# The last shared slot of each block gathered over 112 partitions instead of 128

## The chip, the cores and the metric

The kernel runs on one core of one Trainium2 chip. A time is device microseconds (us) of one execution. The kernel before was run six times: median 799.03 us, lowest 793.24, highest 803.08.

## The reference

Two graph layers run over the same 4096 nodes of 512 features and the same adjacency matrix, which is random with a density of about 1/1024 (four neighbours per node on average). Layer 0 is an attention layer with 8 heads of 64, layer 1 is a mean over the neighbours; each ends in a residual and a layer norm. Cut to what matters:

```python
# layer 0, per head h
Wh = jnp.einsum('nf,hfo->hno', x, W)
f1 = jnp.einsum('hno,ho->hn', Wh, a[:, :F_OUT])
f2 = jnp.einsum('hno,ho->hn', Wh, a[:, F_OUT:])
e = leaky_relu(f1[:, :, None] + f2[:, None, :], 0.2)
e = jnp.where(adj[None] > 0, e, -9e15)
out = jnp.einsum('hnm,hmo->hno', softmax(e), Wh)
x = layernorm(x + out)
# layer 1
agg = mask @ x / max(deg, 1)
combined = concat([x @ W_self + b_self, agg @ W_nb + b_nb])
x = layernorm(x + relu(combined @ W_comb + b_comb))
```

## The kernel before

Nodes are cut into 32 blocks of 128, one node per partition. The kernel never multiplies by the adjacency matrix: it turns each row of it into a list of neighbours and fetches the neighbours' rows from a table in device memory.

**Lists (up to about 225 us of the span).** The adjacency matrix is read block by block. `decode` (L455) turns four blocks at a time into lists. The first three neighbours of each node (K0 = 3) get slots 0 to 2, one row per partition. All further neighbours of a block go, one after the other, into a list shared by the block, of at most 256 entries (KH = 2 times 128): entries 0 to 127 are slot 3, entries 128 to 255 are slot 4, the last shared slot. For each entry the kernel keeps the row to fetch (`idx`), the owner (the node it belongs to, in `es`) and the owner's score part `f1` (`f1s`, copied from PSUM in L523). An entry past the end of its block's list has no owner and fetches row 0 of the table, whose scores are -1e30, so that its weight is zero. Meanwhile the rows of table `t0` (8 scores and 512 features per node) are computed and stored.

**The attention stage (to about 486 us).** For each block, `gather` (L622) issues five indirect DMAs on POOL's queue, one per slot; each fetches one row per partition into the block's tile `g`. All are recorded on L613, the one line of the helper `rows_of` (L612). There are GA = 5 such tiles, each made by `gather_buffer` (L618), so the gathers of block b+5 wait until block b is used up: slot 0 by L668, slots 1 and 2 by L685 on DVE, and slots 3 and 4 by the matmuls of `a_shared` (L697 on PE), which add shared entries to their owners. DVE weighs the rows (L663), ACT scales the sums (L713), makes the layer norm (L728 to L737) and copies what PE made out of PSUM (L351, L746). The products for layer 1 are stored to table `t1` and the transposed features to `xt`.

**The second stage (from about 530 us).** The same lists are used again on rows of `t1`. There are GB = 7 tiles `g`: the five of before and two new ones made at L1078, after the tiles of the list stage were given back. Gathers of blocks 0 to 5 whose rows are ready are issued early (`gather_early`, L629; six late ones follow, `gather_late`, L632). Weights of layer 1 are folded by PE and ACT (`fold_weights`, L296). In the loop, PE multiplies `xT` (reloaded on SP's queue, L769) by the folded weight (`g_self`, L774) and adds the shared slots (`g_shared`, L781); DVE adds slots 1 and 2 (L759, L761) and closes the block (`g_moments`, L797 and L801); ACT makes the norm; SP's queue stores the result (L809). A block's reuse of a tile waits for ACT (slot 0), DVE (1 and 2) and PE (3 and 4).

The order on every engine is the program's order, written by hand. The first tile is made just before the gather of block 0 (L970), the second before that of block 1 (L983), three more before that of block 2 (L987). A test at L1115 sets a flag if some block's shared list is longer than 256 entries; then a dense version of both layers runs after this one.

Of the kernel before, what the change touches and what calls it, by code (L numbers as in the profile page):

```python
# [31 lines left out]
F32 = mybir.dt.float32  # L32
# [4 lines left out]
OP = mybir.AluOpType  # L37
# [3 lines left out]
P = 128  # L41
SLOPE = 0.2
EPS = 1e-5
BIG = 1e30
# [5 lines left out]
K0 = 3  # L50
KH = 2
KS = K0 + KH
KL = 16
KX = KL - K0
GA = 5
GB = 7
NE = 6
# [2 lines left out]
G = 4  # L60
# [26 lines left out]
@with_exitstack  # L87
def kernel(
    ctx: ExitStack,
    tc: tile.TileContext,  # L90
    x: bass.AP,
    adj: bass.AP,
    w0: bass.AP,
    a0: bass.AP,
    w_self: bass.AP,
    b_self: bass.AP,
    w_nb: bass.AP,
    b_nb: bass.AP,
    w_comb: bass.AP,
    b_comb: bass.AP,  # L100
    out: bass.AP,
):
    nc = tc.nc
    flag_pool = ctx.enter_context(tc.tile_pool(name="flag", bufs=1))
    flag = flag_pool.tile([1, 1], I32, name="flag")
    listed_layers(tc, flag, x, adj, w0, a0, w_self, b_self, w_nb, b_nb, w_comb, b_comb, out)
    fl = nc.values_load(flag[0:1, 0:1])
    with tc.If(fl > 0):
        dense_layers(tc, x, adj, w0, a0, w_self, b_self, w_nb, b_nb, w_comb, b_comb, out)
# [3 lines left out]
def listed_layers(  # L113
# [15 lines left out]
    nc = tc.nc  # L129
    N, FIN = x.shape  # L130
    H, _, D = w0.shape
# [6 lines left out]
    TW = H + HD  # L138
# [6 lines left out]
    NC = 32  # L145
    EX = KX + 2 + 1
    AHEAD = (6, 13)
# [8 lines left out]
    const = ctx.enter_context(tc.tile_pool(name="const", bufs=1))  # L156
# [20 lines left out]
    pidx = const.tile([P, KH], F32, name="pidx")  # L177
    nc.gpsimd.iota(
        pidx, [[P, KH]], base=0, channel_multiplier=1, allow_small_or_imprecise_dtypes=True
    )  # L180

    scale = const.tile([P, 1], I32, name="scale")
    nc.gpsimd.iota(scale, [[0, 1]], base=0, channel_multiplier=1)
# [59 lines left out]
    f1s = const.tile([P, NB, KS, H], F32, name="f1s")  # L243
    idx = const.tile([P, NB, KS], U32, name="idx")
    deg = const.tile([P, NB], F32, name="deg")
    end = const.tile([P, NB], F32, name="end")
# [208 lines left out]
    def decode(b0, dp, place):  # L455

        bs = slice(b0, b0 + G)
# [57 lines left out]
        pe = ps.tile([P, G, KH, EX + H], F32, name="sm", bufs=2)  # L515
        for g in range(G):
# [3 lines left out]
                    start=True, stop=True,  # L520
                )
        nc.vector.tensor_copy(es[:, bs], pe[:, :, :, 0:EX])
        nc.vector.tensor_copy(f1s[:, bs, K0:KS, :], pe[:, :, :, EX:])  # L523
        kx = dp.tile([P, G, KH], F32, name="kx", bufs=1)
        nc.vector.tensor_tensor(
            kx, pidx.unsqueeze(1).to_broadcast([P, G, KH]), es[:, bs, :, KX], OP.subtract
        )
        jk = dp.tile([P, G * KH, KX], F32, name="jk", bufs=1)
        nc.vector.tensor_tensor(
            jk, iota[:, 0:KX].unsqueeze(1).to_broadcast([P, G * KH, KX]),  # L530
            kx.rearrange("p g k -> p (g k)").unsqueeze(2).to_broadcast([P, G * KH, KX]),
            OP.is_equal,
        )
        nc.vector.tensor_mul(
            jk, jk, es[:, bs].rearrange("p g k c -> p (g k) c")[:, :, 0:KX]
        )
# [75 lines left out]
    def rows_of(out, table, at):  # L612
        nc.gpsimd.indirect_dma_start(  # L613
            out=out, out_offset=None, in_=table,
            in_offset=bass.IndirectOffsetOnAxis(ap=at, axis=0),
        )

    def gather_buffer(k):  # L618
        pool = ctx.enter_context(tc.tile_pool(name=f"gat{k}", bufs=1))
        return pool.tile([P, KS, TW], F32, name="g")  # L620

    def gather(table, b, g, at=None):  # L622
        for k in range(KS):
            rows_of(
                g[:, k, 0 : table.shape[1]], table, (idx if at is None else at)[:, b, k : k + 1]
            )
        return g

    def gather_early(b, pool):  # L629
        return gather(t1[0 : 2 + min(LE + b, LX) * P, :], b, pool, idxe)  # L630
# [61 lines left out]
    def a_shared(b):  # L692

        for a in range(2):
            r = slice(a * (H + HH), H + HH + a * HH)
            for k in range(KH):
                nc.tensor.matmul(  # L697
                    NM[b][:, a * HD : a * HD + r.stop - r.start],
                    lhsT=OWN[b][:, k, :], rhs=G0[b][:, K0 + k, r],
                    start=False, stop=(k == KH - 1), skip_group_check=True,  # L700
                )
# [225 lines left out]
    for b in range(LB - 1):  # L927
        for k in range(1 + (b in AHEAD)):
            load_x(w + k + XL)
        load_adj(b + 2, ap)  # L930
        if b == 4:
            pads(wp)
        for k in range(2):
            some(lists)
        for k in range(1 + (b in AHEAD)):
            nxt = transposed(w + 1, wp, sums)
            if k == 0 and b in (22, 23, 24):
                transposed(EARLY + b - 22, wp, sums, True)
            if k == 0:
                key_bank(b + 1)  # L940
                for h in range(NH):
                    mask_adj(b + 1, h)
            node_block(w, xT, None if k else b)
            w, xT = w + 1, nxt
        for k in range(2):
            some(lists)
        if b == 16:
            lates = late_lists(dp, fp.tile([P, FB * HD // P, P], F32, name="wr"))
        if b >= 16:
            next(lates, None)  # L950
        if b == 25:
            pieces = mean_row(w_sb, sums, xa)
        if b >= 25:
            next(pieces, None)
        if b % G == G - 1:
            lists = [decode(b + 1 - G, dp, on_own)]
# [11 lines left out]


    gps = [gather_buffer(0)]  # L970
    G0[0] = gather(t0, 0, gps[0])
    mask_adj(LB, 1)
    key_bank(LB + 1)
# [7 lines left out]
    max_keys(LB + 1)  # L981
    ap_cm.__exit__(None, None, None)
    gps.append(gather_buffer(1))  # L983
    G0[1] = gather(t0, 1, gps[1])
    bp_cm.__exit__(None, None, None)
    wq = ctx.enter_context(tc.tile_pool(name="work2", bufs=1))
    gps += [gather_buffer(k) for k in range(2, GA)]  # L987

    def place(c):
# [18 lines left out]
    for k in range(9):  # L1008
        some(lists)
    lists = [decode(NB - G, dp, on_last)]  # L1010
    for k in range(5):
        next(m2s)


    def on(b):
        return 0 <= b < NB
# [3 lines left out]
    for i in range(-3, NB + 2):  # L1020
        if on(i + 1):
            a_shared(i + 1)
        if on(i + 1 + GA):
            G0[i + 1 + GA] = gather(t0, i + 1 + GA, gps[(i + 1 + GA) % GA])
        elif on(i + GA - NB - 1) and i + GA - NB - 1 < GA:
            b = i + GA - NB - 1
            G1[b] = gather_early(b, gps[(NB + b) % GA])
        if on(i + 3):
# [79 lines left out]
    bad = small.tile([P, 4, NB], F32, name="bad", bufs=1)  # L1108
# [3 lines left out]
    )  # L1112
    nc.vector.tensor_scalar(bad[:, 0, :], bad[:, 0, :], FMAX, None, OP.is_gt)
    nc.vector.tensor_scalar(bad[:, 1, :], fmax[:, :, 0], FMAX, None, OP.is_gt)
    nc.vector.tensor_scalar(bad[:, 2, :], end, float(KH * P), None, OP.is_gt)  # L1115
    nc.vector.memset(bad[:, 3, :], 0.0)
    nc.vector.tensor_scalar(bad[:, 3, 0:NE], endl, float(P), None, OP.is_gt)
    nc.vector.tensor_reduce(bsum[:, 0:1], bad.rearrange("p a b -> p (a b)"), AX.X, OP.add)
# [429 lines left out]
```

## Time and profile before

| | us |
|---|---|
| median of six runs | 799.03 |
| lowest and highest | 793.24, 803.08 |
| the profiled execution | 791.82 |
| its span, first to last instruction | 790.1 |
| POOL busy, of it the 326 gathers | 345.0, 311.8 |
| PE, ACT, DVE busy | 627.6, 488.3, 479.0 |
| first and last gather start | 225.70, 749.75 |
| data moved | 209.63 MB, 94.39 MB of it on the queue that POOL fills |

The page is one execution. Its busy times are sums over stages that have different limits, so the stages are read one by one. An instruction's "idle before" is the time its engine did nothing just before it, followed by what ended that. Of the 326 gathers, 160 belong to the attention stage, 30 are early and 6 late ones of the second stage, and 130 belong to blocks 6 to 31 there; every fifth of a block (64 in all) is one of the last shared slot.

### The profile page before, as it was taken

To read this page: it belongs to the slowest core of one execution; us is meant where nothing else is said; L and a number is where in the kernel's file an instruction comes from. 1 tells how busy PE (TensorE), PEld (TensorE's weight loads), DVE (VectorE), ACT (ScalarE), POOL (GpSimd) and SP (SyncE) were. 2 spreads that over 40 slices of the span, in tenths; PEclk is the share of its full clock that TensorE was granted. 3 is DMA by queue.
4 is the path that set the end of the run, shared out by engine and by line. 5 is a ranking of instruction groups with operands and counts; after the bars stand their busy time and mean duration, and the time that the engine had idled before them with its cause. 6 is when DMAs were issued, how large, how long until landed. Compare 5 with 4: busy or idle time off the path is not lost.

```text
span 790.1 us, 8945 instructions
## 1 busy us (share of the span) xinstructions
PE 627.6 (79%) x2229; PEld 351.9 (45%) x2230; DVE 479.0 (61%) x1335; ACT 488.3 (62%) x1236; POOL 345.0 (44%) x410
## 2 busy tenths in 40 slices
PE   5789989978953778799777989767499778987894
PEld 2567666756721344445444545423144333333341
DVE  5267879988851388887967778412026433444463
ACT  3687777887730278798877879731045544555564
POOL 4011111111147266565656652647326666676600
PEclk9899999999956789999999999978599999898997
DMA  8999999998997278789777874857438777887741
GB/s 277 406 408 409 407 408 408 409 409 324 359 299 208 73 198 248 241 292 300 239 246 235 240 227 163 270 173 248 129 96 271 237 264 252 277 258 255 253 141 58
DMA packets 92037, 209.63 MB, mean 265 GB/s; under 512 B 13694, under 2 KB 13702, under 8 KB 91978
## 3 DMA queue, kind: packets, MB, share of 16 engines
q1 hardware_dynamic: 63024, 114.05, 39.3%
q0 software_dynamic: 28624, 94.39, 39.1%
q10 hardware_dynamic: 330, 0.54, 0.2%
q8 instruction: 20, 0.33, 0.2%
q14 instruction: 39, 0.32, 0.1%
HBM read 175.25 MB, written 33.69 MB: 264 GB/s over the span
## 4 chain that ended last, share of the span: by engine, by line
PE 28%; ACT 19%; another core or an unknown queue 10%; issue 8%; DVE 4%; DMA 1%; SPq 0%; ACTq 0%; DVEq 0%
PE nm L774 7%; ACT yp L713 6%; PE pw L774 6%; PE pw L781 3%; PE pw L742 3%; PE nm L781 3%; ACT xs L737 3%; ACT xs L728 2%; PE pw L304 2%; ACT xT L351 2%; PE tp L304 1%; ACT ln_rs L731 1%; DMA xT<-xt 1%; DVE g L663 1%
## 5 line engine op out<-in xcount | busy, mean ns | idle before, releaser
L613 POOL DMA_INDIRECT g<-t,idx x290 | 277.5, 957 | 186.4 <-issue 74.4
L742 PE MATMUL pw<-wr,xT 128*128 128x512 f32 x256 | 126.2, 639 | 26.3 <-ACT xT L351 24.9
L420 ACT ACTIVATE ab<-at 128x2048 bf16<-128x2048 int32 x64 | 122.3, 1912 | 37.2 <-DMA at<-in_adj_dram 33.5
L366 PE MATMUL pw<-w_sb,xT 128*128 128x264 f32 x512 | 132.5, 405 | 11.9 <-DVE sums L355 5.0
L366 PEld LDWEIGHTS pw<-w_sb,xT 128*128 128x128 f32 x512 | 95.4, 196 | 40.9 <-issue 7.0
L663 DVE TENSOR_TENSOR g<-g,ew 128x1024 f32<-128x1024 f32 x64 | 77.4, 1210 | 25.8 <-ACT ew L653 25.4
L742 PEld LDWEIGHTS pw<-wr,xT 128*128 128x128 f32 x256 | 50.6, 204 | 87.9 <-issue 58.9
L377 POOL COPY f1s<-lst 128x24 f32<-128x24 f32 x32 | 7.3, 229 | 178.0 <-DVE fmax L374 95.1
L713 ACT ACTIVATE yp<-num,rd 128x64 f32<-128x64 f32 x256 | 73.1, 286 | 15.0 <-DVE rd L705 4.5
L697 PE MATMUL num<-g,own 128*128 128x264 f32 (+1 forms) x256 | 66.2, 404 | 18.8 <-issue 9.3
L774 PE MATMUL nm<-m,xT 128*128 128x512 f32 x128 | 65.0, 655 | 13.5 <-DMA xT<-xt 9.0
L774 PE MATMUL pw<-m,xT 128*128 128x512 f32 x128 | 62.6, 635 | 10.9 <-DMA xT<-xt 7.3
L797 DVE SCALAR_TENSOR_TENSOR sm<-y,lst,nm 128x512 f32<-128x512 f32 x16 | 12.1, 753 | 93.6 <-PE nm L791 43.4
L697 PEld LDWEIGHTS num<-g,own 128*128 128x128 f32 x256 | 48.3, 198 | 30.5 <-issue 11.9
L774 PEld LDWEIGHTS nm<-m,xT 128*128 128x128 f32 x128 | 26.6, 211 | 49.7 <-issue 33.0
L345 PE MATMUL tp<-ident,xs 128*128 128x128 f32 x256 | 40.8, 284 | 7.6 <-DVE sums L355 7.0
L687 DVE TENSOR_TENSOR num<-num,g 128x512 f32<-128x512 f32 x64 | 44.8, 699 | 2.2
L774 PEld LDWEIGHTS pw<-m,xT 128*128 128x128 f32 x128 | 25.8, 204 | 45.4 <-issue 31.6
L345 PEld LDWEIGHTS tp<-ident,xs 128*128 128x128 f32 x256 | 31.6, 147 | 32.3 <-issue 17.4
L613 POOL DMA_INDIRECT g<-t,idxe x30 | 28.5, 951 | 31.7 <-DVE num L681 12.2
L797 DVE SCALAR_TENSOR_TENSOR sm<-y,lst,pw 128x512 f32<-128x512 f32 x16 | 12.1, 754 | 44.4 <-PE nm L781 12.9
L746 ACT COPY row<-pw 128x512 f32<-128x512 f32 x32 | 18.7, 584 | 31.5 <-remote 21.1
(214 smaller groups left out, 996.9 us busy)
## 6 DMA issues: line engine op xcount, KB each, us to landing
at<-in_adj_dram SPq DMA_DIRECT2D x64, 1024.0 KB
xt<-xT SPq DMA_DIRECT2D x32, 256.0 KB
t<-row SPq DMA_DIRECT2D x32, 256.0 KB
xT<-xt SPq DMA_DIRECT2D x32, 256.0 KB
out_dram<-row SPq DMA_DIRECT2D x32, 256.0 KB
t<-row POOLq DMA_DIRECT2D x31, 260.0 KB
xs<-in_x_dram SPq DMA_DIRECT2D x31, 256.0 KB
g<-t,idx POOLq DMA_INDIRECT x290
```

The source lines that it names most:

```text
L345: nc.tensor.transpose(tp[:, c, :], xs[:, b, ts(c, P)], ident)
L366: nc.tensor.matmul(pw, lhsT=xT[:, c, :], rhs=w_sb[:, c, k * HW : (k + 1) * HW], start=(c == 0), stop=(c == FB - 1),)
L420: nc.scalar.activation(ab, loads.pop((b, h)), AF.Relu, accum_out=asum[:, b, h : h + 1])
L613: nc.gpsimd.indirect_dma_start(out=out, out_offset=None, in_=table, in_offset=bass.IndirectOffsetOnAxis(ap=at, axis=0),)
L663: nc.vector.tensor_tensor(gv, gv, E[b][:, sl].unsqueeze(3).to_broadcast([P, sl.stop - sl.start, H, D]), OP.mult,)
L687: nc.vector.tensor_add(halves_of(NM[b]), halves_of(NM[b]), G0[b][:, k, H:TW].rearrange("p (a c) -> p a c", a=2),)
L697: nc.tensor.matmul(NM[b][:, a * HD : a * HD + r.stop - r.start], lhsT=OWN[b][:, k, :], rhs=G0[b][:, K0 + k, r], start=False, stop=(k == KH ...
L713: nc.scalar.mul(Y[b][:, h * D : (h + 1) * D], NM[b][:, o : o + D], RD[b][:, h : h + 1])
L742: nc.tensor.matmul(pz, lhsT=xT[:, c, :], rhs=m2[:, c, :], start=(c == 0), stop=(c == FB - 1))
L774: nc.tensor.matmul(NM[b], lhsT=xT[:, c, :], rhs=m1[:, c, :], start=False, stop=(c == FB - 1), skip_group_check=True,)
L781: nc.tensor.matmul(NM[b], lhsT=OWN[b][:, k, :], rhs=g[:, K0 + k, 0:HD], start=False, stop=(k == KH - 1), skip_group_check=True,)
L797: nc.vector.scalar_tensor_tensor(yp, Y[b], lst[:, b, KL + 1 : KL + 2], NM[b], OP.mult, OP.add)
```

## The change

The last shared slot is fetched for partitions 0 to 111 only. Its last sixteen rows in each tile are set to zero once, when the tile is made (a memset on POOL of partitions 96 to 127, 520 values each; partitions 96 to 111 are then overwritten by the gathers), and stay zero. The `f1` of those sixteen entries gets -1e30 added, from a small constant tile `void`, so that their weight is zero; the copy of L523 becomes an addition for that. The limit of the test on the shared lists falls from 256 to 240 entries.

```diff
+PL = 112
...
+    void = const.tile([P, KH], F32, name="void")
+    nc.vector.tensor_scalar(void, pidx, float((KH - 1) * P + PL), -BIG, OP.is_ge, OP.mult)
...
-        nc.vector.tensor_copy(f1s[:, bs, K0:KS, :], pe[:, :, :, EX:])
+        nc.vector.tensor_tensor(
+            f1s[:, bs, K0:KS, :], pe[:, :, :, EX:],
+            void.unsqueeze(1).unsqueeze(3).to_broadcast([P, G, KH, H]), OP.add,
+        )
...
     def gather_buffer(k):
         pool = ctx.enter_context(tc.tile_pool(name=f"gat{k}", bufs=1))
-        return pool.tile([P, KS, TW], F32, name="g")
+        g = pool.tile([P, KS, TW], F32, name="g")
+        nc.gpsimd.memset(g[96:P, KS - 1, :], 0.0)
+        return g
 
     def gather(table, b, g, at=None):
         for k in range(KS):
+            p = PL if k == KS - 1 else P
             rows_of(
-                g[:, k, 0 : table.shape[1]], table, (idx if at is None else at)[:, b, k : k + 1]
+                g[0:p, k, 0 : table.shape[1]], table,
+                (idx if at is None else at)[0:p, b, k : k + 1],
             )
         return g
...
-    nc.vector.tensor_scalar(bad[:, 2, :], end, float(KH * P), None, OP.is_gt)
+    nc.vector.tensor_scalar(bad[:, 2, :], end, float((KH - 1) * P + PL), None, OP.is_gt)
```

## The prediction

> **What bounds the kernel now.** I read the page first, then the gathers by stage, then the chain of waits and POOL's timeline inside the longest stage.
>
> ```profile
> PE 627.6 (79%) x2229; PEld 351.9 (45%) x2230; DVE 479.0 (61%) x1335; ACT 488.3 (62%) x1236; POOL 345.0 (44%) x410
> ...
> PE 28%; ACT 19%; another core or an unknown queue 10%; issue 8%; DVE 4%; DMA 1%; SPq 0%; ACTq 0%; DVEq 0%
> ```
>
> By busy share PE looks like the bound and POOL (44%) is idle most of the time; POOL is not even in the chain. Both readings mislead. The gathers alone (L613) by stage; columns are the stretch, its length, POOL busy with gathers, PE's granted clock, DMA share, GB/s:
>
> ```profile
> 0.00:225.00 225.00, 0.00 (x0) 0.97 1.01 382
> 225.00:262.00 37.00, 24.50 (x25) 0.59 0.72 219
> 262.00:486.00 224.00, 129.41 (x135) 0.95 0.75 230
> 486.00:586.00 100.00, 48.45 (x51) 0.83 0.57 179
> 586.00:753.00 167.00, 109.40 (x115) 0.92 0.80 256
> ```
>
> To 225 us the DMA engines are full (share 1.01) with the adjacency matrix, and there are no gathers. From then on a gather takes POOL 0.95 us, and 0.30 us pass before the next starts even when nothing is waited for, so the true pace is 1.25 us: 115 gathers in the last stage need 144 of its 167 us. PE needs less there: the chain shows 3.43 us (L774) and 1.72 us (L781) per block, 5.15, against 5 x 1.25 = 6.27 for a block's gathers. POOL paces that stage. Its pauses, with SP's queue and DVE at the same moment (start, length, instruction, idle before):
>
> ```profile
> 666.62 0.96 POOL L613 DMA_INDIRECT g<-t,idx  x1 [0.30 <-issue]
> ...
> 670.43 0.32 SPq L769 DMA_DIRECT2D xT<-xt  x1
> 670.52 0.76 DVE L797 SCALAR_TENSOR_TENSOR sm<-y,lst,pw 128x512 f32<-128x512 f32 x1 [8.60 <-remote]
> 670.72 0.94 POOL L613 DMA_INDIRECT g<-t,idx  x1 [3.14 <-remote]
> ```
>
> and the chain there:
>
> ```profile
> 657.72 12.72 another core or an unknown queue
> 670.43 2.82 DMA xT<-xt
> ```
>
> SP, DVE and POOL wait for different things and are all released within 0.3 us. What they share is PE's completion signal. The trace's semaphore events show it: from 605 to 736 us POOL runs 15 gathers in a row (18.5 us), pauses 3.1 to 3.25 us, runs 15 again, with a period of 21.7 us (the first of the seven pauses is 2.61 us). While it runs, PE finishes 8 to 14 instructions that signal; of these 0 or 1 arrive in most runs, and the rest arrive together 2.8 to 2.95 us after POOL's last gather. So the "unknown queue" of the chain is PE's signals coming late while POOL issues gathers without a break. The same stands at 259.74 (ACT L308 waits 12.77 us, released 2.2 us after a run of 25 gathers from 225.70 to 257.51) and at 567.26 (after a run of 26). I can't see the cause, only the rule: where POOL runs on, others wait until it stops. POOL's gather time is therefore on the path from 225 to 750 us, whatever its busy share.
>
> **The change, part by part.**
>
> *Does it do what it says?* The flag would send everything through the dense layers if a shared list were longer than 240. Counted from the reference's inputs, the longest of the 32 lists has 227 entries, the next 211. The test costs the same and the dense path stays off: 0 us.
>
> *The list stage.* `void` is one DVE instruction of 2 values per partition; L525 (8 values) takes 162 ns. Eight copies of 64 values (L523, 214 ns each) become additions; the nearest addition (jk, 104 values) takes 268 ns, so at most 0.05 us more each, 0.4 us in all. Most of it lies under the full DMA engines before 225 us, and nobody is recorded as waiting for L523. If uncovered: 0.5 us. I take 0.
>
> *Memsets, five before or inside the first run of gathers.* The rows they are bounded by: a POOL memset of 128 values 0.205 us, of 1 value 0.10, an iota of 512 values 0.56. At 0.8 ns per value 520 values give 0.53 us. The first lies in the 6.6 us that POOL waits for the last row store before 225.70: nothing. The second stands before block 1's gathers, three before block 2's, inside the run from 225.70 to 257.51. Behind them on POOL's queue are 20 gathers, and behind the end of the run waits ACT L308, whose copy PE's weight folding needs, and that is on the chain. So 4 x 0.53 = +2.1 us. Bounds: 0, if the break of 1.6 us lets PE's signals through early (a break of 1.2 us did after runs of six), and 4 x (0.56 + 0.30) = +3.4 with the spacing of the gathers.
>
> *Two more at the second stage's start.* They wait for the list stage's tiles, then stand before block 5's early gathers, which today wait 3.09 us for a row store (to 530.47). That wait hides 1.06 us: 0. If the new tile lies over the layer 1 weight that PE still reads (PE's last such signal is at 530.56), the cover is gone and the run of 26 starts late: +1.1.
>
> *The 64 gathers of 112 rows.* Every gather of the trace has 128 rows, so the price of a row must be bounded. Proportional at best: 0.95/8 = 0.118 us saved each. At the other end POOL's plain DMAs: a store of 128 rows of `t0` (L924) takes 0.54 to 0.57 us, one of a single row (L402) 0.56: rows cost nothing. A gather is 0.41 us dearer than these. If that excess goes with its 128 indices, one eighth is 0.05 us. I take 0.05, between the bounds and nearest to the row that differs only in the indices. A loss isn't excluded either: the slowest gathers (1.33 us at 238.65) are 0.38 us dearer than the others for no reason I see, and no row shows a gather of another size. Five of the 64 (early ones of blocks 0 to 4) stand beside ACT's work; 59 are in runs that others wait for. -59 x 0.05 = -3.0 us; bounds -7.0 and +22.4. Fewer rows also take 64 x 16 x 2 KB = 2.1 MB of 209.6 off the DMA engines, whose share is 0.75 to 0.80 in these stages: not the limit, 0.
>
> The Trainium skill speaks against a saving: "DMA: Bandwidth & Descriptors", section "Anatomy of one DMA — SWDGE (gpsimd) path", puts a POOL DMA's fixed cost at about 2 us and says that many descriptors can be emitted before their cost shows. By that rule alone the 112-row gather saves nothing, and the sum would be +2.1 us instead of -0.9. The plain stores agree with it (0.56 us for 1 row, 0.54 for 128); no run here shows it for gathers.
>
> *Waits.* No gather waits for anything new after a tile's first use: the last slot still waits for PE's shared matmuls. So the runs of 15 and their pauses should stay, each run 3 x 0.05 us shorter.
>
> Sum: 2.1 - 3.0 = -0.9 us. The profiled execution (791.8: span 790.1 and 1.7 outside) would become 790.9; it lies 7.2 us below the median of the six runs, and the same -0.9 on 799.0 gives 798.
>
> **The rivals.**
>
> *Rows cost nothing (15%).* Only the memsets are left: 799.0 + 2.1 = 801. For it: the plain stores. Against it: the gathers' excess of 0.41 us.
>
> *A 112-row gather is dearer than a 128-row one (32%, slower).* One mechanism: POOL makes the descriptors of an odd count less well, at L613, in every run. It decides (over 1%, 8 us) from (8 - 2.1)/59 = +0.10 us per gather. At half the excess of the slowest gather, +0.19, it is 799 + 2.1 + 11.2 = 812; at the full 0.38, 823. For it: nothing in the trace has another count than 128, and the plain DMA of one row is no cheaper than that of 128 (0.56 against 0.54). Against it: 112 is seven eighths of a regular pattern, and descriptors are fewer.
>
> *The runs break up (20%, faster).* If a row is priced in proportion (-7.0 + 2.1 = -4.9) and POOL's lighter load lets PE's signals through inside a run, pauses of 3.14 us vanish; there are seven from 605 to 736. Two gone: 799 - 4.9 - 6.3 = 788; one is enough for 1%. For it: in the runs between 300 and 480 us some signals do arrive inside. Against it: in the long runs almost none does, and the saved time is a few per cent of a run.
>
> **How the numbers follow.** The forecast has 33%. A measurement of this kernel can tell about 1% from no change (the six runs spread from -0.7% to +0.5%). Forecast and "rows cost nothing" lie within 1% (48%); of the dearer gather 4 in 32 stay below +0.10 us, of the broken runs 2 in 20 gain no pause: 54%, from which I move 2 to each side for parts that add up by chance. Slower 28 + 2 = 30%, faster 18 + 2 = 20%, same 50%. The range runs from 787 (two pauses gone, with a little more) to 815 (+0.24 us per gather: 2.1 + 14.2); beyond each end about 1 in 10 is left. Within it, the forecast's own range is 794 (proportional rows) to 803 (rows free, memsets at 3.4, the two late ones uncovered).
>
> **What would show it.** L613 splits into two durations, 0.95 and about 0.90 us for one in five. Two memset groups appear on POOL, four of them between 231 and 241 us, and the chain's restart at 260.38 moves by about 2 us. The rounds of the last stage keep 15 gathers and shrink from 21.7 to 21.5 us. The forecast falls if the 112-row gathers are not cheaper than the others, if the number of gathers between pauses changes, or if PE's signals arrive inside the runs.

## The result

The changed kernel takes 796.06 us (median of 34 runs, 788.58 to 803.01) beside 798.45 us for the kernel before (71 runs, 785.55 to 804.89). The recorded ratio is 1.0005, interval 0.9982 to 1.0028; it leaves out every run more than 1.5% above the fastest of its kernel, and since one run of before took only 785.55 us, that keeps no more than the 23 quickest of its 71. Over all runs the changed kernel is 0.3% below in the medians and 0.4% in the means (795.11 and 798.65). Measured again later, beside the last experiments, it took 792.25 us (12 runs) beside 798.21, ratio 0.9935, interval 0.9904 to 0.9967. So the change is worth less than 1%, and what there is of it is a gain of 0.3 to 0.7%. The kernel's own median moved by 0.5% between the two occasions, so the experiments are compared within one set of runs, made together, where that matters.

The profiled execution of the changed kernel took 793.61 us, its span is 791.8. First the page, with each engine's busy time and the chain of waits by engine:

```profile
PE 632.3 (80%) x2229; PEld 354.8 (45%) x2230; DVE 480.3 (61%) x1336; ACT 488.2 (62%) x1236; POOL 347.4 (44%) x417
...
PE 34%; ACT 15%; issue 9%; another core or an unknown queue 7%; DVE 4%; DMA 1%; SPq 0%; ACTq 0%; DVEq 0%
```

POOL does 7 more instructions (the memsets) and 2.4 us more work. The share of the "unknown queue", which the prediction read as PE's late completion signals, falls from 10 to 7%. The gathers alone by stage, with the edges moved by up to 4 us to follow the later first gather (columns as before: stretch, length, POOL busy, granted clock, DMA share, GB/s):

```profile
229.00:266.00 37.00, 26.63 (x28) 0.75 0.72 212
266.00:487.00 221.00, 126.47 (x133) 0.90 0.75 228
487.00:586.00 99.00, 48.36 (x51) 0.86 0.57 178
586.00:753.00 167.00, 109.04 (x115) 0.92 0.80 251
```

The last stage is as it was: 115 gathers, 109.0 us instead of 109.4. The first stretch isn't: 28 gathers fit where 25 did, and in the 34 us from the first gather on PE is busy for 28.5 us instead of 15.2. POOL's timeline in that stretch (start, length, instruction, idle before) shows what is new:

```profile
234.53 0.94 POOL L620 DMA_INDIRECT g<-t,idx  x1 [0.30 <-issue]
235.47 0.55 POOL L628 MEMSET g<- 32x520 f32 x1
236.18 0.96 POOL L620 DMA_INDIRECT g<-t,idx  x1 [0.16 <-issue]
...
241.44 0.94 POOL L620 DMA_INDIRECT g<-t,idx  x1 [0.30 <-issue]
242.36 1.50 POOL L628 MEMSET g<- 32x520 f32 x3
244.02 0.96 POOL L620 DMA_INDIRECT g<-t,idx  x1 [0.16 <-issue]
```

The three memsets before block 2's tile keep the next gather back for 1.65 us after 242.37. Beside them, ACT's copies in the weight folding, from the timeline of the same stretch (L297 copies a piece of the weight that PE has turned, L312 a folded piece; they are L293 and L308 of before):

```profile
243.73 0.58 ACT L297 COPY row<-yp 128x512 f32<-128x512 f32 x1 [2.27 <-PE yp L296]
248.58 0.58 ACT L312 COPY wr<-pw 128x512 f32<-128x512 f32 x1 [4.26 <-PE pw L308]
...
257.33 0.58 ACT L312 COPY wr<-pw 128x512 f32<-128x512 f32 x1 [3.06 <-issue]
```

The same copies in before:

```profile
238.54 0.58 ACT L293 COPY row<-yp 128x512 f32<-128x512 f32 x1 [11.41 <-PE yp L292]
246.38 0.58 ACT L293 COPY row<-yp 128x512 f32<-128x512 f32 x1 [7.26 <-issue]
259.74 0.58 ACT L308 COPY wr<-pw 128x512 f32<-128x512 f32 x1 [12.77 <-remote]
```

There the first folded piece (L308) was copied at 259.74, 34.0 us after the first gather; here (L312) at 248.58, 19.2 us after it. PE's signal gets through in the gap, 1.34 us after the end of the gather before it, and the folding runs beside the gathers that follow.

The pauses of the last stage stayed:

```profile
666.75 0.95 POOL L620 DMA_INDIRECT g<-t,idx  x1 [0.30 <-issue]
...
670.66 0.32 SPq L780 DMA_DIRECT2D xT<-xt  x1
670.76 0.75 DVE L808 SCALAR_TENSOR_TENSOR sm<-y,lst,pw 128x512 f32<-128x512 f32 x1 [7.50 <-PE nm L792]
...
670.95 0.94 POOL L620 DMA_INDIRECT g<-t,idx  x1 [3.26 <-PE nm L792]
```

Again SP, DVE and POOL are released within 0.3 us. From 627 to 711 us four rounds of 15 gathers stand as before; a fifth, to 733 us, has a pause of 0.75 us behind its third gather. The round ahead of them broke into 11 and 4, and the last gathers into 5 and 7. The 112 rows aren't needed for a break into 11 and 4: the profiles of three kernels that gather 128 rows throughout (memsets alone, memsets on DVE, additions alone, all below) have it too.

And the gathers of 112 rows: in the trace's instruction list their median is 0.935 us, that of the same slot in before 0.946; from start to start 1.240 us against 1.251. A gather of 112 rows saves POOL 0.011 us, not 0.05, and the gather behind it (slot 0 of the next block) takes 0.953 us instead of 0.946, which gives most of that back.

So the nearly equal time may hide a difference. The theory from these views: **the breaks that the memsets make help, and something else in the change takes part of that back.** The rival: nothing of it matters, and the two profiles differ by chance.

### The profile page after: what moved, and what is told of

It reads as the page before. It is cut to its first block, busy times and chain, and to the rows that moved or that the text cites. A ratio compares the mean times of both kernels' runs of the same rounds, so it can differ in the third digit from the quotient of the medians.

```text
span 791.8 us, 8938 instructions
## 1 busy us (share of the span) xinstructions
PE 632.3 (80%) x2229; PEld 354.8 (45%) x2230; DVE 480.3 (61%) x1336; ACT 488.2 (62%) x1236; POOL 347.4 (44%) x417
## 4 chain that ended last, share of the span: by engine, by line
PE 34%; ACT 15%; issue 9%; another core or an unknown queue 7%; DVE 4%; DMA 1%; SPq 0%; ACTq 0%; DVEq 0%
PE pw L785 7%; PE nm L785 6%; PE pw L753 6%; ACT yp L724 4%; PE nm L792 3%; PE num L708 3%; PE pw L792 3%; PE tp L308 2%; ACT xs L748 2%; ACT xs L739 2%; ACT xT L355 1%; DVE g L674 1%; DVE num L698 1%; DMA xT<-xt 1%
## 5 line engine op out<-in xcount | busy, mean ns | idle before, releaser
L753 PE MATMUL pw<-wr,xT 128*128 128x512 f32 x256 | 132.1, 664 | 30.2 <-ACT xT L355 28.8
L424 ACT ACTIVATE ab<-at 128x2048 bf16<-128x2048 int32 x64 | 122.3, 1912 | 38.0 <-DMA at<-in_adj_dram 35.4
L370 PE MATMUL pw<-w_sb,xT 128*128 128x264 f32 x512 | 134.2, 409 | 11.5 <-DVE sums L359 5.0
L753 PEld LDWEIGHTS pw<-wr,xT 128*128 128x128 f32 x256 | 52.7, 213 | 96.2 <-issue 61.4
L620 POOL DMA_INDIRECT g<-t,idxe x30 | 28.5, 949 | 31.2 <-DVE num L682 12.9
L374 DVE COPY row<-pw 128x264 f32<-128x264 f32 x64 | 26.8, 422 | 21.4 <-PE pw L370 16.4
```

Of the source, the lines that this page charges most:

```text
L370: nc.tensor.matmul(pw, lhsT=xT[:, c, :], rhs=w_sb[:, c, k * HW : (k + 1) * HW], start=(c == 0), stop=(c == FB - 1),)
L374: nc.vector.tensor_copy(row[:, k * HW : (k + 1) * HW], pw)
L424: nc.scalar.activation(ab, loads.pop((b, h)), AF.Relu, accum_out=asum[:, b, h : h + 1])
L620: nc.gpsimd.indirect_dma_start(out=out, out_offset=None, in_=table, in_offset=bass.IndirectOffsetOnAxis(ap=at, axis=0),)
L753: nc.tensor.matmul(pz, lhsT=xT[:, c, :], rhs=m2[:, c, :], start=(c == 0), stop=(c == FB - 1))
```

## The experiments

### The two halves of the change

The memsets alone, on the kernel before:

```diff
-        return pool.tile([P, KS, TW], F32, name="g")
+        g = pool.tile([P, KS, TW], F32, name="g")
+        nc.gpsimd.memset(g[96:P, KS - 1, :], 0.0)
+        return g
```

> The kernel before with the seven memsets alone; all gathers keep 128 rows. Theory (a break in POOL's run lets PE's completion signals through): the three memsets before block 2's gathers make a break of about 1.6 us near 240 us; PE's signals arrive in it, ACT's wait of 12.8 us that ended at 259.7 is gone from that place, and the time is 0 to 3 us below the kernel before (ratio 0.996 to 1.000). Rival (memsets only push the queue back): the wait stays, the end of the first run moves by 2.1 us, ratio 1.0025.

Measured: 787.86 us beside 798.21, ratio 0.9887, interval 0.9841 to 0.9934. Faster, by about 10 us in the medians, where the theory had 0 to 3. POOL's longer break and ACT beside it:

```profile
240.10 0.95 POOL L613 DMA_INDIRECT g<-t,idx  x1 [0.30 <-issue]
...
241.05 1.49 POOL L621 MEMSET g<- 32x520 f32 x3
...
242.50 0.58 ACT L293 COPY row<-yp 128x512 f32<-128x512 f32 x1 [1.57 <-DMA g<-t,idx]
...
242.71 0.95 POOL L613 DMA_INDIRECT g<-t,idx  x1 [0.16 <-issue]
...
247.15 0.58 ACT L308 COPY wr<-pw 128x512 f32<-128x512 f32 x1 [4.07 <-PE pw L304]
```

The first folded piece is copied 19.1 us after the first gather (228.09), as in the changed kernel.

The rest alone: the changed kernel without memsets, each tile's first use over 128 rows (so that nothing unwritten is read), every later one over 112.

```diff
-        nc.gpsimd.memset(g[96:P, KS - 1, :], 0.0)
...
+    used = set()
...
-            p = PL if k == KS - 1 else P
+            p = PL if k == KS - 1 and id(g) in used else P
...
+        used.add(id(g))
```

> The changed kernel without memsets: the first gather into each tile has 128 rows (its last sixteen entries fetch row 0, which leaves zeros), every later one of the last slot 112. Theory (a 112-row gather saves POOL only 0.011 us): 59 x 0.011 = 0.65 us, ratio 0.999, and ACT's wait of about 12.8 us that ends near 260 us is there again, because nothing breaks the first run. Rival (rows matter, in POOL's time or in traffic): 3 to 7 us less, ratio 0.991 to 0.996.

Measured: 808.17 us, ratio 1.0127, interval 1.0064 to 1.0190. Slower, which neither the theory nor the rival had. So the change is a sum of effects of opposite sign, each of about 1% when measured alone.

### What a row and what a gather cost

The changed kernel without memsets, and in the second stage slot 3 over 64 rows and slot 4 over 16 (the rows left out are not fetched, so the result isn't that of the reference):

```diff
-            p = PL if k == KS - 1 else P
+            p = {3: 64, 4: 16}.get(k, P) if id(g) in used and table.shape[1] == HD else P
```

> No memsets; attention stage as before; in the second stage slot 3 is gathered over 64 rows and slot 4 over 16, after the first use of a tile; the rows left out are not fetched, so the shared neighbours beyond them are not those of the reference. Theory (POOL's time per gather hardly depends on its rows: 0.0007 us per row by 128 against 112): 0.90 us for 64 rows and 0.87 for 16, 0.12 us per block, 23 blocks, 2.8 us less, ratio 0.996; the rounds of 15 gathers stay. Rival 1 (proportional POOL time): 0.47 and 0.12 us, some 30 us less, ratio 0.96. Rival 2 (the second stage is paced by its data): 27% fewer gathered bytes there, 20 us or more less, ratio 0.975 or lower, with POOL's durations unchanged.

Measured: 797.43 us, ratio 1.0034, interval 0.9992 to 1.0075. POOL's timeline in a round of the last stage, slots 3 and 4 being the shorter ones:

```profile
643.11 0.91 POOL L620 DMA_INDIRECT g<-t,idx  x1 [0.30 <-issue]
644.32 0.86 POOL L620 DMA_INDIRECT g<-t,idx  x1 [0.31 <-issue]
645.49 0.96 POOL L620 DMA_INDIRECT g<-t,idx  x1 [0.30 <-issue]
```

The medians are 0.946 us for 128 rows, 0.910 for 64 and 0.862 for 16 (and 0.935 for 112, above). Between 128 and 16 rows that is 0.084 / 112 = 0.00075 us a row, on some 0.85 us that every gather costs. The Trainium skill, "DMA: Bandwidth & Descriptors", section "Anatomy of one DMA — SWDGE (gpsimd) path", says that many descriptors can be emitted before their incremental cost shows; these four sizes agree, and for this term that rule, which the prediction set aside for the nearest row, was nearly right. Fewer bytes bring nothing either, as the prediction said: the time is that of before, and even the 2.8 us that the theory took from POOL's shorter instructions don't show.

The last shared slot left out of the second stage (its matmul reads slot 3 once more, so this result isn't the reference's either):

```diff
-        for k in range(KS):
+        for k in range(KS if table.shape[1] == TW else KS - 1):
...
-                NM[b], lhsT=OWN[b][:, k, :], rhs=g[:, K0 + k, 0:HD],
+                NM[b], lhsT=OWN[b][:, k, :], rhs=g[:, K0, 0:HD],
```

> The kernel before with the last slot's gathers left out of the second stage (its matmul reads slot 3 again, so its share of the neighbours is not the reference's); POOL issues four gathers per block there instead of five. Theory (POOL's number of gathers paces that stage): 23 blocks on the path x 1.25 us = 29 us less, less what PE (5.15 us per block against 4 x 1.25 = 5.0) then holds back; 20 to 32 us less, ratio 0.960 to 0.975. Rival (PE or the DMA engines pace it and POOL is idle 56% anyway): at most 5 us less, ratio 0.994 or above.

Measured: 759.75 us, ratio 0.9515, interval 0.9458 to 0.9572, that is 38 us. The gathers from the restart of the loop to the last one, first before, then this kernel (stretch, length, POOL busy with gathers, clock, DMA share, GB/s):

```profile
586.70:750.70 164.00, 109.40 (x115) 0.92 0.80 257
```

```profile
585.42:720.86 135.44, 87.33 (x92) 1.00 0.83 266
```

23 gathers fewer, 28.6 us less: 1.24 us each, the pace of POOL's gathers. The miss is one of size: 20 to 32 us were expected, from these 23. The other nine count too: from the first early gather to the restart of the loop, where they were left out, it takes 88.0 us instead of 98.0. All 32 at 1.25 us make 40, near the 38 measured. PE's matmuls stay the same in number, but its granted clock is 1.00 instead of 0.92, which may have helped. So POOL does pace that stage, as the prediction had it, by the number of its gathers and not by their rows.

### Is it the break?

The same seven memsets with gathers of 128 rows, but on DVE, so that POOL has no break:

```diff
-        nc.gpsimd.memset(g[96:P, KS - 1, :], 0.0)
+        nc.vector.memset(g[96:P, KS - 1, :], 0.0)
```

> The kernel before with the seven memsets of the change, but on the vector engine (DVE) instead of GpSimd (POOL); all gathers keep 128 rows. With the memsets on POOL the ratio was 0.989. Theory (what helps is the break of 1.65 us that three memsets make in POOL's stream of gathers, in which the completion signals of PE get through): no break, the first run of about 25 gathers is whole again (31.8 us in the profile of before), ratio 0.997 to 1.003, so 796 to 801 us. Rival (what helps is in the tiles: an earlier first writer, other waits of the first gathers or of PE): ratio 0.985 to 0.993 here too, 786 to 793 us.

Measured: 800.38 us, ratio 1.0042, interval 1.0004 to 1.0081: the gain is gone, with a little more. ACT's copies of the folding, from the timeline:

```profile
242.34 0.58 ACT L293 COPY row<-yp 128x512 f32<-128x512 f32 x1 [14.90 <-remote]
...
251.43 0.58 ACT L293 COPY row<-yp 128x512 f32<-128x512 f32 x1 [8.51 <-issue]
...
261.26 0.58 ACT L308 COPY wr<-pw 128x512 f32<-128x512 f32 x1 [9.24 <-remote]
```

POOL's first run is 25 gathers long again, from 225.83 to 257.26. Two copies of turned pieces (L293) stand inside it, as in before, but the first folded piece (L308) comes 4.0 us behind its end, 35.4 us after the first gather. The rival (an earlier writer of the tiles, other waits) falls.

If the break is what helps, more of them should help where the other long run stands. Four more were put into the run of 26 gathers, on the kernel with the memsets alone; each writes three times over rows that the next gathers overwrite:

```diff
+    def pause(g):
+        for k in range(3):
+            nc.gpsimd.memset(g[96:P, KS - 1, :], 0.0)
...
+    pause(gps[NE])
     for b in range(NE):
         gather_late(b, gl)
+    pause(gps[NE])
...
+        pause(gps[b])
         G1[b + GB] = gather(t1, b + GB, gps[b])
```

> The kernel of the memsets alone (0.989) with four more breaks of three memsets each (about 1.65 us) in the run of 26 gathers that POOL issues at 530 to 563 us of the profile of before: ahead of the gathers of the late rows, behind them, and ahead of blocks 7 and 8. Theory (PE's signals get through only where POOL's gathers pause): the waits of ACT for the folded weights (6.4, 8.5 and 8.6 us in before) shrink, the stretch from the last early gather to the restart of the second stage's loop (59 us from 527.4 to 586.7) becomes 46 to 53 us, and the kernel 6 to 13 us faster than the 787.9 us of the memsets alone: ratio 0.971 to 0.980. Rival (the breaks only lengthen POOL's stream): four times 1.65 us, but hidden in the 23.7 us in which POOL waits for the restart: ratio 0.987 to 0.997.

Measured: 775.71 us beside 796.61, ratio 0.9757, interval 0.9702 to 0.9813. Of the three other kernels of that set none is under 797. The chain of waits in order of time, from 541 us of before:

```profile
541.99 0.58 ACT row L293
542.58 6.40 another core or an unknown queue
548.97 0.02 issue
549.00 0.59 ACT m L308
549.58 8.57 another core or an unknown queue
```

and of the kernel with the breaks:

```profile
542.83 0.59 ACT m L308
543.42 0.04 issue
543.46 3.71 PE tp L304 x8
547.18 0.02 issue
547.20 0.59 ACT m L308
547.79 0.04 issue
547.84 3.70 PE tp L304 x8
```

Where before has a hole between two copies, PE's own matmuls stand now, and the "unknown queue" is out of the chain from there to 567 us. The loop's first gather of block 9 starts 39.3 us after the run's first gather instead of 56.2, although each of the four breaks keeps POOL from its gathers for 1.9 to 2.0 us. In these 39.3 us PE is busy for 36.1 at a granted clock of 1.00, in the 56.2 of before for 38.3 at 0.82, so most of what shrank is waiting. The stretch that the expectation gave as 46 to 53 us (59.3 in before) takes 41.1 (526.00 to 567.10). This is the fastest of the kernels that fetch all that before fetches: 20.9 us under it, with the same gathers. The same memsets on another engine were tried for the first run only, not for these four breaks.

### What takes the gain back

Three kernels and a repetition, none with memsets. First the additions on DVE alone, every gather over 128 rows (an edit of the changed kernel):

```diff
-        nc.gpsimd.memset(g[96:P, KS - 1, :], 0.0)
...
-            p = PL if k == KS - 1 else P
+            p = P
```

> The kernel before with only the additions on the vector engine (the void mask, the addition of it to the scores of the shared slots, the limit of 368): no memsets, every gather over 128 rows. Theory (the gathers of 112 rows, by their shape or by what they change in the order of signals, make the 1.0 to 1.3 per cent that the rows-only kernel lost): ratio 0.997 to 1.003. Rival (the additions on the vector engine, or another choice of waits that they bring, make the loss): ratio 1.008 to 1.018, 804 to 812 us.

Measured: 800.05 us, ratio 1.0038, interval 1.0000 to 1.0076.

Then 112 rows in the attention stage only, by a further condition on the rows-only kernel, `and table.shape[1] == TW`:

> As the rows-only kernel (void mask, first use of each tile over 128 rows, no memsets), but 112 rows only for the last slot of the blocks gathered in the attention stage (27 of the 64 gathers); the second stage gathers 128 rows throughout. Theory (the loss arises in the attention stage, since 64 and 16 rows in the second stage had cost only 0.3 per cent): ratio 1.008 to 1.018. Rival (the loss comes from the second stage, or from gathers of 112 rows in proportion to their number, 27 of 59): ratio 1.000 to 1.006.

Measured: 797.85 us, ratio 1.0016, interval 0.9983 to 1.0050. The theory missed: no loss there. Then in the second stage only, with `== HD` in its place:

> As the rows-only kernel, but 112 rows only for the last slot of the blocks gathered in the second stage; the attention stage gathers 128 rows, and there are no memsets. Theory A (the attention-rows kernel has only 0.2 per cent, so the loss of the rows-only kernel sits here): ratio 1.007 to 1.016. Theory B (no loss in either stage): 1.000 to 1.006.

Measured: 801.83 us, ratio 1.0039, interval 1.0002 to 1.0077. No loss beyond that of the additions. And the rows-only kernel once more:

> The rows-only kernel of the first call (1.0127), unedited. Theory A (its loss belongs to the kernel): 1.008 to 1.018 again. Theory B (it was scatter, or that chip): 1.000 to 1.006, as the void-only kernel (1.0038) and the attention-rows kernel (1.0016).

Measured: 804.63 us, ratio 1.0082, interval 1.0043 to 1.0121. The loss is the kernel's own, at two thirds of its first size. Each part of it alone costs 0 to 0.4%; together they cost 0.8 to 1.3%. Some of it lies in the second stage: both profiles of this kernel have 60.7 and 60.1 us from block 5's first gather to the restart of the loop (before 56.2) and 166.4 and 166.3 us from there to the end of the last gather (before 164.0). Why the parts add up to more than their sum isn't shown, and such stretches vary: the kernel with the memsets on DVE, which gathers 128 rows, has 59.0 in the first of them.

With the memsets in place, the changed kernel with 128 rows in every gather (the edit of `p` above, nothing else):

> The changed kernel with its memsets and its additions on the vector engine, but with every gather over 128 rows: against the changed kernel of the same call it isolates the 112 rows in the presence of the breaks. Theory A (the gathers of 112 rows cost about one per cent, as the first call's two kernels imply): ratio 0.988 to 0.994, the changed kernel 1.0 per cent above it. Theory B (a gather of 112 rows costs nothing, 64 times 0.011 us are saved; the loss lies in the additions on the vector engine or in scatter between builds): ratio within 0.4 per cent of the changed kernel's.

Measured: 789.11 us, ratio 0.9899, interval 0.9856 to 0.9941. And the changed kernel itself in the same set:

> The changed kernel itself, unedited, beside the others of this call. Ratio to before expected 0.998 to 1.003, as measured earlier.

Measured: 792.25 us, ratio 0.9935, interval 0.9904 to 0.9967: outside its expectation. Against the kernel of 128 rows it is 3.1 us slower (12 runs and 6; the ratio of their means, worked out from these runs, is 1.0036, interval 1.0009 to 1.0063). So 112 rows don't save 3 us here, they cost about 3: a third of the 1% of theory A, and within the 0.4% that theory B allowed, though the interval leaves out 0. Why, no row shows: POOL's instruction is shorter, and in single profiles the attention stage of one kernel differs by more than this from run to run (before 263.0 us; others with the same gathers and no memsets 262.8 to 271.7). That stays open.

### The stage that decides, over all kernels

One number separates the fourteen profiles without overlap: from the first gather's start to the end of the 26th, the first that must wait for a tile to be used up.

| kernel | us |
|---|---|
| memsets on POOL: changed kernel, twice | 34.5, 34.5 |
| memsets on POOL, 128 rows: memsets alone, all 128, more breaks | 34.5, 34.8, 34.6 |
| none on POOL: before, memsets on DVE | 45.2, 45.9 |
| none on POOL: rows only, twice | 39.9, 46.2 |
| none on POOL: 64 and 16 rows, last slot left out | 39.5, 40.0 |
| none on POOL: additions only, attention rows, second-stage rows | 39.8, 45.7, 45.6 |

The 112 rows leave no mark in it: 34.5 us with them, 34.5 to 34.8 without. Breaks of 0.71 and 1.65 us (one memset, then three) save 5 to 12 us there; which of the two does more wasn't tried. In the profiles at 39.9 (rows only) and 39.8 (additions only) a folded piece is copied inside the run without any break, at 251.19 and 254.71: now and then a signal gets through by itself. The whole attention stage (to the first early gather) takes 255.6 to 261.4 us with the memsets on POOL and 262.8 to 273.6 without. The profiled execution of before, with 263.0, was among the shortest of its kind, and the whole execution 7 us under the median. So the two profiles side by side, 263.0 and 259.7 us, show 3.3 us of a gain of about 10.

## Why the prediction was right, and where it was not

The forecast was 798 us, the measured time 796.06 and later 792.25; "within 1%" was right both times. It was right as a sum and wrong in both its terms, whose errors had opposite signs. That was luck, not an understanding of the kernel.

- **The four memsets in the first run, +2.1 us: the step that failed.** The duration was right (0.53 us foreseen, 0.554 measured in the mean of seven). The effect measured alone is -10.4 us (787.86 against 798.21). The prediction named the condition itself, "if the break of 1.6 us lets PE's signals through early", and priced it as 0 at best: the four memsets' own cost avoided. It didn't price what the signals release, although it had read the wait of 12.77 us of ACT L308 a few paragraphs earlier. The bound should have gone down by as much as that wait.
- **The two memsets at the second stage's start, 0: right.** They ran at 527.82 and 528.29, inside the wait for the row store; the next gather starts at 530.93, in before at 530.47.
- **The 64 gathers, -3.0 us: wrong, in size and in sign.** By POOL's own time 59 x 0.011 = -0.6 us, most of it lost again in the gather behind each; measured in the kernel, about +3 us. The 0.05 us rested on the thought that the excess of a gather over a plain DMA (0.41 us) goes with its indices. It goes with the instruction: 16 rows still cost 0.86. The rival "rows cost nothing" was right on the price of a row; the rival "dearer" was right on the sign of this term, but its mechanism (a dearer gather at L613) is refuted.
- **"The runs break up": what it describes happened, in another place and for another reason.** It was given 20% and put down to cheaper rows in the rounds of the last stage. The run that broke was the first one, by the memsets. Four of the last stage's rounds stayed whole, 18.49 to 18.51 us long where before had 18.50 to 18.56, so they hardly shrank either.
- **POOL paces the second stage, DMA bytes don't: right.** 23 gathers fewer took 28.6 us off, while 64 and 16 rows in place of 128, with the traffic from the restart to the last gather down from 257 to 208 GB/s, took off nothing.
- **List stage and flag, 0:** the flag stayed off. The additions measured alone are 1.0038, with 1.0000 as the interval's end: not told apart from 0.
- **The reading of the "unknown queue" as PE's late signals: right** as far as tried: it is what the two break experiments rest on, and in the kernel with more breaks the queue is out of that part of the chain.
- **A slip without weight:** 5 x 1.25 is 6.25 us, not 6.27.

## What to carry to other kernels

Where one engine issues small indirect DMAs without a break and others show waits that end together just after it stops, count what a gap in that stream would release, not only what it costs: here gaps of 0.71 and 1.65 us brought some 10 us, and four more of 1.9 to 2.0 us another 12 (787.86 to 775.71 us, from two sets of runs). Cut the number of gathers, not their rows. And when a change adds and removes, run each half alone: the small total here was -1.1% from one half and, measured alone, +0.8 to +1.3% from the other, and the half that helps can be had alone.

## What the runs showed that was not expected

- PE's completion signals aren't late from the start of a run of gathers. In the run of 26 of before, from 530.47 us, the signals recorded up to 540.76 come within 0.02 us of PE's end, as the trace's semaphore events show; late ones follow after that, the last at 567.26, 4.25 us behind the run's last gather. In the kernel with more breaks the first four runs there are 6.0 to 7.2 us long, and all fourteen signals recorded from 528 to 567 us come within 0.02 us of PE's end, inside the runs (538.43, 547.18, 554.13) as well as in the breaks. So a break seems to help by keeping the run short, and memsets on POOL can fill it. Whether the length of a run, the number of its gathers or something that drains in the break decides wasn't tried.
- A gather costs POOL 0.85 us and 0.00075 us a row (128, 112, 64 and 16 rows: 0.946, 0.935, 0.910 and 0.862 us).
- In the changed kernel seven memsets of 32 x 520 on POOL took 0.554 us each in the mean, and back to back they start 0.47 us apart.
